# Placing the previous image's steps by hand in a two-layer FNO and dilation kernel

## The chip, the core and the metric

The kernel runs on one core of one Trainium2 chip. The metric is device time in microseconds (us) of one execution. Four runs of the kernel before the change took 3962.23 to 3968.06 us, with a median of 3965.28 us.

## The reference

`x` has 8 images of 8 channels and 256 x 256 pixels, in float32. The channels form 4 groups of 2 (`G` = 4). Two residual layers are applied:

```python
x = x + L0(_gn(x))                    # _gn: normalise each image by groups of 2 channels
x = x + max_3x3(_gn(x))               # dilation, the border counts as -2

def L0(x):                            # a Fourier neural operator, separate for each of 4 groups
    h = gconv1x1(concat(x, gridx, gridy), fc0_w, fc0_b)       # 4 -> WID = 10 channels per group
    for i in range(4):
        xf = rfft2(h)
        # keep 24 rows kx (12 lowest, 12 highest) x 12 columns ky; mix the 10 channels at each mode
        h1 = irfft2(einsum(xf_kept, sp_w1[i] or sp_w2[i]))
        h = h1 + gconv1x1(h, w_w[i], w_b[i])
        if i < 3: h = gswish(h, betas[i])                     # h * sigmoid(h * softplus(beta)) / 1.1
    h = gswish(gconv1x1(h, fc1_w, fc1_b), betas[3])           # 10 -> 128 channels per group
    return gconv1x1(h, fc2_w, fc2_b)                          # 128 -> 2 channels per group
```

## The kernel before

**Two streams of work.** All matmuls are float32. Image by image the program does a latent part, `layers(b, ...)`, which holds the state `h` (30 rows of each 32 partitions in use, 11 chunks of 4 x 512 columns) in SBUF, and a head, `head(b, ...)`, which reads the last state back from DRAM and applies fc1, the activation and fc2. The head of image b-1 is cut into 128 steps (`STEPS`), which are laid between the pieces of the latent part of image b; the head of the last image runs alone at the end. The dilation of a finished image is a third, thin stream of pieces, called tails here (`dilate`, lines 730 to 766).

**A head step.** `first(n)` (L674) makes 4 matmuls (8 instructions, L680) into 4 PSUM banks, and ACT applies Silu to them in two instructions (L681, one bank; L682, three banks). Every odd step also calls `second(n - 3)` (L685): 8 matmuls (16 instructions, L702) over the activations of steps n-3 and n-2 into one bank, which DVE adds to the output `y` (L707, or L705 for the first of a block). Before a block of three steps, `load_state` (L667) has SP fetch a chunk of the state; at the first pair of a block of 16, SP fetches `y` (L695); after the last pair POOL writes `y` to DRAM (L715). A tail is a few DVE instructions on two rows (L748 to L764); its input `yin` comes and its output goes by POOL's queue.

**PSUM.** Two pools share the 8 banks: `one` (2 buffers of one bank) and `tri` (2 buffers of three banks). A step takes one of each, an odd step a second `one`; so does nearly every piece of the latent part, by `ps_a`, `ps_tri` or `ps_four` (both).

**A layer of the latent part.** `spectrum_h` (L341): four DVE transposes (L347) turn the gathered coefficients `zt`, then 96 matmul instructions make `p_b` (L356), and DVE scales it into `B` (L363). `mix` (L376): twelve DVE instructions of 800 elements, alternately a multiplication (L383) and a reduction (L386), mix the channels at each mode; two more make `F`; matmuls fold the result (`p_f`, L403) and four copies of 32 partitions each put it into the diagonal places of `fz` (L416 to L419, by `copy`, L196, which gives every second copy to ACT while no head exists). `rows_of` (L421): matmuls turn `fz` into row coefficients (`p_g`, L435 or L440) and ten copies bring them into `zt`. `layer` (L458): for each of 11 chunks `burst` (L504) adds the 1x1 convolution (L511 or L514) and the inverse transform (L517) in 4 banks, and ACT writes the chunk back (L522, or L524 in the last layer). In layers 0 to 2 the chunks are taken in pairs k: `turn` (L461) transposes a chunk on DVE in two halves (L465), `transform(k)` (L472) makes `p_d` from a pair (L482; copied out by DVE, L485, and ACT, L486), and `gather(k)` (L488) makes `p_u` (L496) and copies it into `zt` (L499, L502). In layer 3 nothing is turned, and SP writes each chunk to DRAM (`stored`, L526).

**The next image's start.** `spectrum_x` (L242) normalises x and computes its spectrum with a DFT by matmuls: `p_a` (L283, L289, L296), then `p_xs` (L307), where 64 small matmuls (128 instructions) unfold the half spectrum, group by group, into 4 banks. `mix(b + 1, 0)` follows. These form `start(b + 1)`; layer 3 of image b advances it by one yield at each `next(side)` (L455, L544, L546), and what is then left runs at the image's end (L608).

**What sets the order.** PE, DVE and ACT run in program order (`manual_schedule`, L789); SP and POOL issue DMAs in an order that the scheduler picks. In the main loop (L796 to L813) each yield of the latent part says what goes in there. A tuple is an exact number of steps. A plain number is a weight: it is scaled (L814) so that an image has 128 steps, and a step is placed when the shares add up to one. `"odd"` and `"even"` insert a step when the parity is wrong. `"tail"` places one tail. A head is created after the whole of `layers(b)`, the start of b+1 included (L820).

Of the kernel before, what the change touches and what calls it, by code (L numbers as in the profile page):

```python
# [21 lines left out]
G = 4  # L22
# [21 lines left out]
def fno_dilate_kernel(ctx: ExitStack, tc: tile.TileContext, a: dict, out: bass.AP):  # L44
# [78 lines left out]
    nc.vector.memset(fz, 0.0)  # L123

# [117 lines left out]
    def spectrum_x(b, out_):  # L242
# [36 lines left out]
        a1, a2, a3 = turned[:, 2, 0:512], turned[:, 2, 512:1024], turned[:, 2, 1024:1072]  # L279
# [18 lines left out]
        nc.vector.tensor_copy(a3, p[:, 0:48])  # L298
        yield
        yield  # L300
        a3 = a3.rearrange("p (j k) -> p j k", j=2)
        one, tri, banks = ps_four(f"p_xs_{b}")
        for k in range(2):
            for term in range(2):
                for q in range(4):
                    for g in range(G):
                        mm(banks[g][part(q), 6 * k : 6 * k + 6], unf[part(g), spectrum_table(k, term), :],  # L307
                           a3[part(g), :, 12 * term + 3 * q : 12 * term + 3 * q + 3],
                           start=term == 0, stop=term == 1)
        xe4 = xe.rearrange("p (s k) g j -> p s g j k", s=2)  # L310
        for k in range(2):
            nc.vector.tensor_copy(
                xe4[:, k, 0, 0:2, :], one[:, 6 * k : 6 * k + 6].rearrange("p (j k) -> p j k", j=2))
            nc.vector.tensor_copy(
                xe4[:, k, 1:4, 0:2, :], tri[:, :, 6 * k : 6 * k + 6].rearrange("p g (j k) -> p g j k", j=2))
# [25 lines left out]
    def spectrum_h(b, l, out_):  # L341
# [3 lines left out]
        for g in range(G):  # L345
# [3 lines left out]
            yield 1.2  # L349
# [26 lines left out]
    def mix(b, l, out_):  # L376
# [3 lines left out]
        for k in range(3):  # L380
            for k2 in range(2):
                pr = turned[:, 2, 1024 * k2 : 1024 * k2 + 800].rearrange("p (g m i) -> p g m i", g=G, i=WID)
                nc.vector.tensor_tensor(  # L383
                    pr, sw[k], bt[:, k2, k].unsqueeze(2).to_broadcast([128, G, 2 * WID, WID]), ALU.mult)
                yield 0.7
# [4 lines left out]
                if k == 0 and k2 == 1:  # L390
                    sw.append(load_sw(l, 2))
                yield 0.7
# [3 lines left out]
        yield 0.5  # L396

        yield "odd"
        p = ps_tri(f"p_f_{b}_{l}")[:, 0, :]
        for slot in range(2):  # L400
            for n, (table, part_of) in enumerate(((0, slot), (1 + slot, 1 - slot))):
                for q in range(4):
                    mm(p[part(q), 120 * slot : 120 * slot + 120], fold[part(q), table, :],  # L403
                       f[part(q), part_of].rearrange("p k g o -> p (k g o)"), start=n == 0, stop=n == 1)
# [11 lines left out]
        for q in range(4):  # L416
            dst = fz[part(q), :, :, 6 * q : 6 * q + 6].rearrange("p o g k -> p k g o")
            src = p[part(q), :240].rearrange("p (k g o) -> p k g o", g=G, o=WID)
            copy(q, dst, src)  # L419

    def rows_of(b, l, side):  # L421
# [3 lines left out]
        for os_ in (range(0, 4), range(4, 8), range(8, 10)):  # L425
# [25 lines left out]
            yield (1, 1) if os_[0] == 0 else (1,)  # L451
            if l < 3:
                yield "tail"
            elif os_[0] < 8:
# [3 lines left out]
    def layer(b, l, out_, stored, side):  # L458
# [79 lines left out]
        if l == 3:  # L538
            yield "odd"
            for c in range(NCH):  # L540
# [4 lines left out]
                yield (1,)  # L545
                next(side, None)  # L546
            return
        yield "even"
        for k in range((NCH + 1) // 2):
            c = 2 * k  # L550
            burst(c)
            if k > 1:
                gather(k - 2)
            if alone[0]:
                turn(c)
                if c + 1 < NCH:
# [3 lines left out]
                if c + 1 < NCH:  # L560
                    turn(c + 1)
                yield (1, 1)
                continue
            yield (1,)
            turn(c, (0,))
            if k > 0:
                transform(k - 1)
            turn(c, (1,))
            yield "tail"
            if c + 1 < NCH:  # L570
                burst(c + 1)
                turn(c + 1, (0,))
                yield (1,)
                turn(c + 1, (1,))
                yield "tail"
            else:
                yield (1,)
# [3 lines left out]
        yield 2  # L581
        gather(k)
        yield 1

    def start(b, out_):
        if b < n_img:
            out_["sw"] = [load_sw(0, 0), load_sw(0, 1)]
            yield from spectrum_x(b, out_)
            for i, n in enumerate(mix(b, 0, out_)):
                if isinstance(n, str):  # L590
                    yield n
                elif i % 2:
                    yield 1.4

    def layers(b, stored, d, then):
# [4 lines left out]
        for l in range(4):  # L600
# [6 lines left out]
            yield from layer(b, l, d, stored, then)  # L607
        yield from then  # L608
# [51 lines left out]
    def head(b, stored, stats):  # L660
# [58 lines left out]
        load_state(1)  # L719
# [270 lines left out]
```

## Time and profile before

| what | value |
|---|---|
| median of 4 runs | 3965.28 us |
| the profiled execution's own time | 3965.84 us |
| its span, first to last instruction | 3964.0 us |
| PE busy | 3673.8 us (93%) |
| ACT busy | 2832.7 us (71%) |
| DVE busy | 2457.7 us (62%) |
| PE weight loads (PEld) | 1432.9 us (36%) |
| POOL busy | 117.0 us (3%) |

The first `p_f` of image 1 starts at 362.0 us; up to there no head runs. From image to image the same point then comes after 471.8, 472.8, 472.8, 472.9, 474.1 and 476.9 us. The last chunk of image 7 ends at 3653.8 us, and the remaining head steps and the last dilation take the last 310 us.

In a busy column a matmul that is held back by a PSUM bank in the middle of its group is counted as busy, so PE's 93% holds waiting too. The timeline shows it as a group that takes longer than the same group elsewhere.

### The profile page before, as it was taken

To read this page: it belongs to the slowest core of one execution; us is meant where nothing else is said; L and a number is where in the kernel's file an instruction comes from. 1 tells how busy PE (TensorE), PEld (TensorE's weight loads), DVE (VectorE), ACT (ScalarE), POOL (GpSimd) and SP (SyncE) were. 2 spreads that over 40 slices of the span, in tenths; PEclk is the share of its full clock that TensorE was granted. 3 is DMA by queue.
4 is the path that set the end of the run, shared out by engine and by line. 5 is a ranking of instruction groups with operands and counts; after the bars stand their busy time and mean duration, and the time that the engine had idled before them with its cause. 6 is when DMAs were issued, how large, how long until landed. Compare 5 with 4: busy or idle time off the path is not lost.

```text
span 3964.0 us, 118698 instructions
## 1 busy us (share of the span) xinstructions
PE 3673.8 (93%) x53882; PEld 1432.9 (36%) x53882; DVE 2457.7 (62%) x3740; ACT 2832.7 (71%) x2933; POOL 117.0 (3%) x202
## 2 busy tenths in 40 slices
PE   5667999999999999999999999999999999999997
PEld 2333333333333333333433333333333333333222
DVE  6664656556765666756666576665776566763633
ACT  2434777777777777777777777776777767778886
POOL 1000000000000000000000000000000000000100
PEclk8888999999999999999999999999999999999998
DMA  3014111432215221251222512134211432215311
GB/s 86 15 35 173 54 32 49 138 124 68 61 56 178 88 68 59 82 188 56 61 65 96 190 48 60 59 131 147 67 53 55 169 107 60 67 49 190 100 52 47
DMA packets 114128, 345.05 MB, mean 87 GB/s; under 512 B 16040, under 2 KB 18536, under 8 KB 98200
## 3 DMA queue, kind: packets, MB, share of 16 engines
q1 hardware_dynamic: 95432, 276.32, 22.1%
q0 software_dynamic: 18192, 61.13, 4.6%
q8 instruction: 424, 6.95, 0.7%
q14 instruction: 80, 0.66, 0.1%
HBM read 213.39 MB, written 123.74 MB: 85 GB/s over the span
## 4 chain that ended last, share of the span: by engine, by line
PE 74%; DVE 13%; ACT 6%; issue 5%; DMA 1%; POOL 0%; SPq 0%; DVEq 0%; POOLq 0%; ACTq 0%
PE p_fc L680 19%; PE p_fc L702 19%; PE p_z L517 9%; PE p_d L482 7%; PE p_z L514 7%; ACT h L522 3%; PE p_z L511 2%; PE p_b L356 2%; DVE turned L347 2%; PE p_u L496 2%; DVE turned L465 2%; PE p_g L435 2%; PE p_g L440 2%; DVE S L386 2%; DVE y L707 2%
## 5 line engine op out<-in xcount | busy, mean ns | idle before, releaser
L682 ACT ACTIVATE act<-p_fc 128x1536 f32<-128x1536 f32 x1024 | 1492.0, 1457 | 2.9 <-PE p_fc L680 2.9
L680 PE MATMUL p_fc<-hs,c_w 32*128 32x512 f32 x8192 | 1166.0, 630 | 12.9 <-DVE h L705 6.1
L702 PE MATMUL p_fc<-act,c_w 128*32 128x512 f32 x8192 | 990.9, 601 | 0.4 <-issue 0.4
L681 ACT ACTIVATE act<-p_fc 128x512 f32<-128x512 f32 x1024 | 615.5, 601 | 450.8 <-PE p_fc L680 439.9
L465 DVE STREAM_TRANSPOSE turned<-h 128x1024 f32<-128x1024 f32 x528 | 646.9, 1234 | 290.0 <-ACT h L522 290.0
L522 ACT ACTIVATE h<-p_z 128x512 f32<-128x512 f32 (+1 forms) x528 | 511.9, 1021 | 261.6 <-PE p_z L517 261.6
L680 PEld LDWEIGHTS p_fc<-hs,c_w 32*128 32x128 f32 x8192 | 387.6, 185 | 551.2 <-ACT act L681 209.6
L707 DVE TENSOR_TENSOR y<-p_fc,y 128x512 f32<-128x512 f32 x392 | 266.2, 679 | 445.9 <-PE p_fc L702 445.9
L702 PEld LDWEIGHTS p_fc<-act,c_w 128*32 128x32 f32 x8192 | 215.5, 109 | 705.9 <-issue 395.8
L517 PE MATMUL p_z<-c_binv,zt 32*128 32x256 f32 x5632 | 410.7, 406 | 3.1 <-ACT zt L198 1.8
L514 PE MATMUL p_z<-h,c_wt 32*32 32x512 f32 x8448 | 388.3, 603 | 18.4 <-DVE zt L200 7.7
L517 PEld LDWEIGHTS p_z<-c_binv,zt 32*128 32x128 f32 x5632 | 259.1, 187 | 312.1 <-issue 298.5
L482 PE MATMUL p_d<-turned,c_fw 32*32 32x480 f32 (+1 forms) x9216 | 327.8, 541 | 17.3 <-DVE zt L499 5.1
L524 ACT ACTIVATE h<-p_z,c_bias 128x512 f32<-128x512 f32 (+1 forms) x176 | 186.6, 1111 | 108.0 <-PE p_z L517 107.7
L486 ACT ACTIVATE turned<-p_d 128x1440 f32<-128x1440 f32 x144 | 183.1, 1271 | 107.4 <-PE p_d L482 104.2
L200 DVE COPY zt<-p_g 128x264 f32<-128x264 f32 x300 | 162.0, 616 | 90.8 <-PE p_g L435 50.4
L482 PEld LDWEIGHTS p_d<-turned,c_fw 32*32 32x32 f32 x9216 | 127.3, 103 | 212.6 <-issue 64.4
L386 DVE TENSOR_REDUCE S<-turned 128x80 f32<-128x800 f32 x192 | 188.8, 984 | 5.2
L383 DVE TENSOR_TENSOR turned<-t,B 128x800 f32<-128x800 f32 x192 | 188.4, 981 | 1.2 <-DMA t<-in_spw 1.0
L347 DVE STREAM_TRANSPOSE turned<-zt 128x960 f32<-128x960 f32 x96 | 174.5, 1852 | 1.8
L514 PEld LDWEIGHTS p_z<-h,c_wt 32*32 32x32 f32 x8448 | 96.5, 103 | 214.4 <-ACT act L681 70.8
L485 DVE COPY turned<-p_d 128x480 f32<-128x480 f32 x144 | 88.6, 615 | 137.6 <-PE p_d L482 136.7
(179 smaller groups left out, 1991.4 us busy)
## 6 DMA issues: line engine op xcount, KB each, us to landing
stored<-h SPq DMA_DIRECT2D x88, 1024.0 KB
hs<-stored SPq DMA_DIRECT2D x352, 256.0 KB
t<-in_spw SPq DMA_DIRECT2D x96, 400.0 KB
yin<-y_rows POOLq DMA_DIRECT2D x56, 512.0 KB, 5.2
h<-in_xp SPq DMA_DIRECT2D x352, 48.0 KB
turned<-in_xw SPq DMA_DIRECT2D x16, 1024.0 KB
y<-in_x SPq DMA_DIRECT2D x56, 256.0 KB
y_rows<-y POOLq DMA_DIRECT2D x56, 256.0 KB, 2.3
```

The costliest lines, as they stand in the source:

```text
L347: nc.vector.transpose(rows[:, 960 * g : 960 * (g + 1)].rearrange("p (i r) -> p i r", r=32), windows(g))
L386: nc.vector.tensor_reduce(s[k2][:, k].rearrange("p g s o -> p (g s o)"), pr.rearrange("p g m i -> p (g m) i"), AX.X, ALU.add,)
L465: nc.vector.transpose(dst[:, 2 * i : 2 * i + 2], h[:, c, 2 * i : 2 * i + 2].rearrange("p f (s x) -> p f s x", s=2))
L482: mm(banks[q][part(v % 4), : 240 * n], fw8[part(q), v, :], t[part(q), :, :, v, : NBLK * WID], start=v < 4, stop=v >= 4)
L514: mm(o, wt[part(q), l, g, :], h[part(q), c, f, :], start=True, stop=False)
L517: mm(banks[q][:, HW * s : HW * (s + 1)], zt[part(q), 2 * c + s].rearrange("p f o -> p (f o)"), binv[part(q), :], start=False, stop=s == 1)
L522: nc.scalar.activation(dst, src, AF.Silu)
L680: mm(banks[g], w1[part(g), blk, :], hs[k][part(g), :], start=True, stop=True)
L681: nc.scalar.activation(act[:, 0, :], one, AF.Silu)
L682: nc.scalar.activation(act[:, 1:4, :], tri, AF.Silu)
L702: mm(acc[part(g), :], w2[:, g, 15 - rb - i : 47 - rb - i], act[:, g, :], start=i == 0, stop=i == 1)
L707: nc.vector.tensor_tensor(y, sums, y, ALU.add)
```

## The change

All weights and parity yields become fixed numbers of steps, and the head of an image is created as soon as its last layer ends, before the rest of `start(b + 1)`, with its first two loads issued at once. Steps per layer, before (as the trace shows them, images 2 to 7) and after (counted in the code):

| stretch | layers | before | after |
|---|---|---|---|
| from `p_f` to the first burst | 0, 1, 2 / 3 | 7, 7, 7 / 6 | 7, 7, 7 / 6 |
| first burst to last burst | 0, 1, 2 / 3 | 10, 10, 10 / 20 | 8, 8, 8 / 20 |
| last burst to `p_b` | 0, 1, 2 | 8, 7, 7 | 8, 8, 8 |
| `p_b` to the next `p_f` | 0, 1, 2 | 9, 8, 8 | 9, 9, 9 |
| last burst of layer 3 to the next image's `p_f` | 3 | 4 | 6 |

The steps keep their parity at each of these places. In layers 0 to 2 the first pair of chunks has no step and no tail between its pieces; in the later pairs both halves of the even chunk are turned before `transform`, and the tails (two, in pairs 2 to 4) stand behind it. In the twelve mixing instructions a step follows each but the numbers 2, 6 and 10. A layer 3 has tails in two places per chunk for six chunks, and one of its two `next(side)` in `rows_of` moves behind the last group of copies. The four copies into `fz` become one multiplication with a mask `own` over all partitions, with `p_f` laid out in `fz`'s order and taken from pool `one`. The 64 unfolding matmuls become 16, from an operand `a3` of 128 rows that holds each group's values in its own 32 rows and zeros elsewhere; the result fills one bank of pool `one`.

```diff
+    own = const.tile([128, NQ], F32, tag="own", name="own")
+    nc.vector.memset(own, 0.0)
+    for i in range(NQ):
+        nc.vector.memset(own[part(i), i : i + 1], 1.0)
...
-        a1, a2, a3 = turned[:, 2, 0:512], turned[:, 2, 512:1024], turned[:, 2, 1024:1072]
+        a1, a2 = turned[:, 2, 0:512], turned[:, 2, 512:1024]
+        a3 = turned[:, 2, 1024:1216].rearrange("p (g m) -> p g m", g=G)
+        nc.vector.memset(a3, 0.0)
...
-        nc.vector.tensor_copy(a3, p[:, 0:48])
+        for g in range(G):
+            nc.vector.tensor_copy(a3[part(g), g, :], p[part(g), 0:48])
...
-        one, tri, banks = ps_four(f"p_xs_{b}")
+        p = ps_a(f"p_xs_{b}")
         for k in range(2):
             for term in range(2):
                 for q in range(4):
-                    for g in range(G):
-                        mm(banks[g][part(q), 6 * k : 6 * k + 6], unf[part(g), spectrum_table(k, term), :],
-                           a3[part(g), :, 12 * term + 3 * q : 12 * term + 3 * q + 3],
-                           start=term == 0, stop=term == 1)
+                    k0 = 12 * term + 3 * q
+                    mm(p[part(q), 24 * k : 24 * k + 24], unf[:, spectrum_table(k, term), :],
+                       cols[:, :, :, k0 : k0 + 3], start=term == 0, stop=term == 1)
...
-            yield 1.2
+            yield (1,) if g < G - 1 else (1, 1)
...
+            if l > 0:
+                if n not in (2, 6, 10):
+                    yield (1,)
+            elif n % 2 or n > 7:
+                yield (1,)
...
-        yield "odd"
-        p = ps_tri(f"p_f_{b}_{l}")[:, 0, :]
+        p = ps_a(f"p_f_{b}_{l}")
...
-        for q in range(4):
-            dst = fz[part(q), :, :, 6 * q : 6 * q + 6].rearrange("p o g k -> p k g o")
-            src = p[part(q), :240].rearrange("p (k g o) -> p k g o", g=G, o=WID)
-            copy(q, dst, src)
+        nc.vector.tensor_tensor(
+            fz[:, :, :, : 6 * NQ].rearrange("p o g (q k) -> p (o g) q k", q=NQ),
+            p[:, : 6 * WID * G].rearrange("p (n k) -> p n k", k=6).unsqueeze(2).to_broadcast([128, WID * G, NQ, 6]),
+            own.unsqueeze(1).unsqueeze(3).to_broadcast([128, WID * G, NQ, 6]), ALU.mult)
...
-            yield (1, 1) if os_[0] == 0 else (1,)
+            yield (1, 1) if os_[0] == 0 or os_[0] == 8 and l < 3 else (1,)
             if l < 3:
                 yield "tail"
-            elif os_[0] < 8:
+            elif os_[0] != 4:
                 next(side, None)
...
-            if alone[0]:
+            if k == 0 or alone[0]:
                 turn(c)
...
-                yield (1, 1)
                 continue
             yield (1,)
-            turn(c, (0,))
-            if k > 0:
-                transform(k - 1)
-            turn(c, (1,))
-            yield "tail"
-            if c + 1 < NCH:
+            turn(c)
+            transform(k - 1)
+            for _ in range(2 if k > 1 and pair else 1):
+                yield "tail"
+            if pair:
                 burst(c + 1)
                 turn(c + 1, (0,))
-                yield (1,)
+            yield (1,)
+            if pair:
                 turn(c + 1, (1,))
-                yield "tail"
-            else:
-                yield (1,)
         out_["sw"] = [load_sw(l + 1, 0), load_sw(l + 1, 1)]
         gather(k - 1)
         transform(k)
-        yield 2
+        yield (1,)
         gather(k)
-        yield 1
...
             yield from layer(b, l, d, stored, then)
+        yield "stored"
         yield from then
...
         load_state(0)
         load_state(1)
+        yield
...
+                if n == "stored":
...
+                    heads.append((b, head(b, stored, stats_of[b])))
+                    next(heads[-1][1])
+                    alone[0] = False
+                elif n == "tail":
+                    tail()
+                elif heads:
+                    for _ in n:
                         step()
```

## The prediction

> **What bounds the kernel now.** The page comes first: busy shares, then the chain that ended last.
>
> ```profile
> PE 3673.8 (93%) x53882; PEld 1432.9 (36%) x53882; DVE 2457.7 (62%) x3740; ACT 2832.7 (71%) x2933; POOL 117.0 (3%) x202
> ...
> PE 74%; DVE 13%; ACT 6%; issue 5%; DMA 1%; POOL 0%; SPq 0%; DVEq 0%; POOLq 0%; ACTq 0%
> ```
>
> PE is the bound in images 1 to 7 and DVE is what it waits for. The number of steps doesn't change, so only PE's waiting can move. The waits by releaser, then the timeline of PE and of DVE, say where it waits:
>
> ```profile
> PE p_f L403 <- DVE F L394: 97.1, 18, 15.5
> PE p_b L356 <- DVE turned L347: 40.9, 22, 7.5
> ...
> PE p_z L514 <- DVE zt L200: 7.7, 6, 1.3
> ```
>
> ```profile
> 1534.08 3.75 PE L356 MATMUL p_b<-turned,c_eh_f 128*32 128x120 f32 x96 [1.56 <-DVE turned L347]
> ...
> 1582.88 1.04 PE L680 MATMUL p_fc<-hs,c_w 32*128 32x512 f32 x8
> 1583.85 1.92 PE L702 MATMUL p_fc<-act,c_w 128*32 128x512 f32 x16
> 1585.71 1.16 PE L514 MATMUL p_z<-h,c_wt 32*32 32x512 f32 x32
> ...
> 1695.92 1.15 PE L514 MATMUL p_z<-h,c_wt 32*32 32x512 f32 x30 [1.29 <-DVE zt L200]
> ...
> 1751.12 2.54 PE L514 MATMUL p_z<-h,c_wt 32*32 32x512 f32 x31
> ...
> 1779.43 1.02 PE L403 MATMUL p_f<-F,c_fold 32*32 32x120 f32 x32 [4.13 <-DVE F L394]
> ...
> 1840.37 2.16 PE L482 MATMUL p_d<-turned,c_fw 32*32 32x480 f32 x60 [0.66 <-DVE zt L502]
> ```
>
> ```profile
> 1692.34 2.46 DVE L248 BATCH_NORM_STATS2 bn_x<-turned 128x6 f32<-128x512 f32 x4
> 1694.72 1.05 DVE L200 COPY zt<-p_g 128x264 f32<-128x264 f32 x2
> ...
> 1875.18 0.75 DVE L705 SCALAR_TENSOR_TENSOR y<-p_fc,c_b,y 128x512 f32<-128x512 f32 x1 [2.75 <-PE p_fc L702]
> 1875.85 3.68 DVE L347 STREAM_TRANSPOSE turned<-zt 128x960 f32<-128x960 f32 x2
> ...
> 1903.53 0.69 DVE L707 TENSOR_TENSOR y<-p_fc,y 128x512 f32<-128x512 f32 x1 [0.49 <-PE p_fc L702]
> 1904.13 0.27 DVE L394 TENSOR_TENSOR F<-S,S 128x120 f32<-128x120 f32 x1
> ```
>
> The starts of 1582.88 to 1585.71 give a step's price on PE: 0.97 us for the first part, 1.86 for the second, so an odd step costs 2.83. The DVE rows show the cause of most waits: DVE runs in order, an odd step's add (0.69) can't start before PE's second part ends, and everything behind it waits (at 1875.18 DVE stood idle for 2.75 us with four transposes queued).
>
> **The change part by part**, per image unless said; plus is faster. Where steps move between stretches, each is credited at its PE price, so the terms add up.
>
> *Last burst to `p_b`.* From `p_u` of pair 4 to `p_b` layer 0 now takes 16.05 us (1867.82 to 1883.87) with 6 first parts and 3 second parts, layers 1 and 2 take 14.6 (1519.50 to 1534.08) with 5 and 2. Now a step stands before the first transpose, and its add holds all four back. After, none does: `p_u` 0.95, `p_d` 1.4, a step 0.97, `p_u` 0.6, then five steps (4.85 + 3 x 1.86 = 10.4) and 0.5 for ACT, whose two instructions (601 + 1457 ns) are slower than a step's PE part: 14.8 with 6 and 3. DVE needs a copy 0.41, four transposes of 1.85 and two adds, 9.2, beside the 10.4. Gain 1.25 + 2 x (14.6 + 2.83 - 14.8) = 6.5; bounds 4 (`p_b` waits 0.8 in each) and 7.
>
> *Mixing, `p_b` to `p_f`.* Now the last add stands right before `F`: 16.95 us from the end of `p_b` (1887.6 to 1904.56) in layer 0, 16.35 and 17.3 in layers 1 and 2. After, four odd steps end at 4 x 3.96 = 15.85 (a pair of steps by the L680 starts 1887.53, 1891.50, 1895.49), the add of the last runs to 16.6, and behind it stand two mixing instructions (1.95) and `F` (0.5): `p_f` at 19.1, with only one even step to cover it. Layer 0 loses 2.15; layers 1 and 2, which take one first part more, lose 1.75 and 0.8: -4.7. Bounds -6 and -3.5. So part of what is won before `p_b` comes back before `p_f`.
>
> *Pairs 1 to 5.* At 1840.37 a tail of five DVE instructions stood between the last half transposition and the copies of `p_u`, so `p_d` waited. Summed over the 84 such places, the step ahead of `p_d` advances 20.0 us more than 0.97 each. The moved tails leave the copies first: +2.6 of 2.86; lower bound 1.5.
>
> *First pair without steps.* Now from the first `p_z` to the end of `p_d` of pair 0 takes 15.1 us, of which 4.8 are steps. After, three bursts run at ACT's pace (2.05 each), one step follows, and `p_d` waits for the second chunk's transposes to 9.1: 11.2 with 1.0 of steps. Nothing gained, nothing lost; what was a wait for ACT becomes one for DVE.
>
> *Folding.* Four copies take 2.3 us; one multiplication of 960 elements 1.15 (between 981 ns for L383's 800 and 1201 for L748's 1024). Beside steps this shows little: `p_f` leaves pool `tri`, whose bank held the next step (1.1 us in layer 1), but the second part now waits for the multiplication to free `one`. `p_f` to `p_g`: 5.95, 5.35, 4.9 become 5.1 each: +0.7 (0 to 0.9). In image 0 ACT and DVE take the copies in turn with nothing beside them: 4 x 1.2 = 5 once.
>
> *Rows of layer 3.* Four bn_stats (2.46) stood before the last copies; behind them the first burst starts at 1693.8, not 1695.9: +2.1 in six images.
>
> *Unfolding.* The burst behind it took 2.54 where 1.15 is free, since `p_xs` held a `tri` bank: that goes. The nearest row for the new form is L440 (128 instructions of 128x32 by 66 columns in 1.98 us), 0.5 for 32; the other end is today's 1.66. So the burst ends at 1751.1 to 1752.3, not 1753.7: +1.8 (1.4 to 2.6), six images. DVE's memset and three more copies (about 0.2 each, from L298's 207 ns) stand beside steps. Against this stands the Trainium skill, "TensorEngine Tiling (Array Packing)", "Performance Considerations": tile the rows where the contraction is 32, up to 4x, and don't count on fewer columns below 60. By it a quarter of the matmuls at a quarter of the concurrency would save nothing, and the term would be 1.4, and the gain 2 us less in all; no row shows this form at 24 columns.
>
> *More tails in layer 3* may hold a `one` bank: -0.5.
>
> *Hand-over.* The new head's five steps come among the last four mixing instructions and `F`. From the last burst (1767.1): second parts of steps 124 and 126 to 4.8, step 0 to 5.8; step 1 needs the bank of step 126's sum, whose add stands behind five mixing instructions, so it waits to 10.2; `p_f` comes at 18.1 instead of 12.3, and with seven steps in `rows_of` the next layer's first burst at 40.3 instead of 36.8. That is 3.5 later with 2 first parts and 1 second part more (3.8): 0, bounds -5 and +3. What is queued: SP's loads of a new head are no risk, since SP's timeline has the first issued at 1757.9 for a step at 1786.8, and the stored chunks lie in DRAM long before; the load of `y` must wait until POOL has written the last block (add, 0.69, issue 0.54, landing 2.3) and lands about when it is needed. In image 0 the 7.7 us between last burst and `p_f` take five steps: +3 once. Image 7 has no start: three steps fewer run alone, +0.7.
>
> **The sum**: 7 x (6.5 - 4.7 + 2.6 + 0.7) = 35.7; 6 x (2.1 + 1.8 - 0.5) = 20.4; 5 + 3 + 0.7 = 8.7: 65 us. The profiled execution's own time is 3965.84 (span 3964.0), 0.6 above the median: 3965.8 - 65 = 3901, against the median 3900. With all lower bounds (the tails of layer 3 at -1) the gain is 7 x (4 - 6 + 1.5) + 6 x (2.1 + 1.4 - 1 - 5) + 5 = -14, 3979; with all upper ones 7 x (7 - 3.5 + 2.9 + 0.9) + 6 x (2.1 + 2.6 + 3) + 8.7 = 106, 3859. The terms are independent, so this case's own range is 3868 to 3938.
>
> **Rivals.** *A. The hand-over stalls* (bank, `y`, two second parts in a row): 5.5 us in six images, 3933 to 3940. For: DVE's add is 5 us behind PE there. Against: PE waits 4.13 there already. *B. Nothing is gained*: the copies, adds and transposes only wait elsewhere, as in the first pair, and the mixing loses 6: 3965. Against: 2.1 and 1.8 are tied to single banks and instructions. *C. Slower.* In pairs 2 to 4 two tails now stand together between `p_d`'s copy and the odd chunk's transposition, 63 places. DVE has 3.05 us there (copied at 7.35, ACT done at 10.4 after the pair's start) and two tails take 2.4 to 3.3, more if `yin` (5.2 us to landing) is late; the transposition, the add and the next `p_d` then slip. It decides from 65 / 63 = 1.03 us a place; at 1.6 the time is 4000. Against: behind the transposes `p_d` has another 1.3 us. That the steps move as the code says leaves no doubt.
>
> **How the numbers follow.** Forecast 0.62, A 0.13, B 0.07, C 0.18. A change of 0.2% (8 us) is about what a measurement of this kernel can tell. Faster is the forecast and A, 0.75; same 0.07; slower 0.18. For 8 in 10 the range goes from the forecast's low end over A and B into C's weak end: 3866 to 3985.
>
> **What would show it.** Right: `p_b` no longer waits for `turned`; `p_f` in the mixing waits about 2.2 us for `F` in every layer; the burst behind `p_xs` takes 1.2; 472.8 us an image become about 464. Wrong: `p_d` waiting for `turned` in pairs 2 to 4, or over 45 us from the last burst to the next image's first.

## The result and the profile after

The changed kernel takes 3974.6 us (median) against 3968.1 us for the kernel before in the same comparisons: ratio 1.0019, 95% interval 1.0014 to 1.0025. The prediction was 3900 us. About 70 us of expected gain are missing. The profiled execution's own time is 3972.05 us, its span 3970.2 us.

First the busy time and the chain that ended last, from the page of the changed kernel:

```profile
PE 3680.4 (93%) x53114; PEld 1427.2 (36%) x53114; DVE 2442.7 (62%) x3675; ACT 2829.5 (71%) x2923; POOL 117.0 (3%) x202
...
PE 79%; DVE 11%; issue 4%; ACT 4%; DMA 2%; POOL 0%; DVEq 0%; SPq 0%; POOLq 0%; ACTq 0%
```

PE has 768 instructions less than before and is busy 6.6 us longer. Something that PE does has become slower; this is the first thing to look for. Then the waits of the changed kernel by releaser (us in total, times, longest):

```profile
PE p_f L415 <- DVE F L405: 86.0, 27, 13.1
...
PE p_d L494 <- DVE turned L477: 23.2, 18, 1.4
...
PE p_fc L686 <- DVE y L713: 21.4, 6, 9.4
...
DVE turned L390 <- DMA t<-in_spw: 18.9, 8, 7.3
...
PE p_b L362 <- DVE turned L353: 15.0, 2, 7.5
...
PE p_z L523 <- DVE wcn L549: 14.1, 7, 3.4
```

`p_b` waits only in image 0 now, as forecast. `p_f` waits almost as long as before, but as 27 waits instead of 18: the hand-over's 4.13 us are gone and each mixing has 2.13 us instead. Two lines were in no forecast: the first burst of layer 0 waits for `wcn`, and a mixing instruction on DVE waits for a DMA, the spectral weights. That a step waits for an add on `y` was in the hand-over's term, as a wait of 4.4 us (5.8 to 10.2); it takes 1.2 to 9.4.

Last the timeline of PE, then of DVE, around one mixing (layer 3, image 3), and the same place by windows (the column after the engines is the granted clock of TensorE):

```profile
1667.00 1.14 PE L686 MATMUL p_fc<-hs,c_w 32*128 32x512 f32 x8
1670.27 1.96 PE L415 MATMUL p_f<-F,c_fold 32*32 32x120 f32 x32 [2.13 <-DVE F L405]
1672.16 1.85 PE L686 MATMUL p_fc<-hs,c_w 32*128 32x512 f32 x8
```

```profile
1667.14 0.75 DVE L711 SCALAR_TENSOR_TENSOR y<-p_fc,c_b,y 128x512 f32<-128x512 f32 x1 [0.66 <-PE p_fc L708]
1667.80 0.98 DVE L390 TENSOR_TENSOR turned<-t,B 128x800 f32<-128x800 f32 x1
1668.82 0.99 DVE L393 TENSOR_REDUCE S<-turned 128x80 f32<-128x800 f32 x1
1669.84 0.28 DVE L405 TENSOR_TENSOR F<-S,S 128x120 f32<-128x120 f32 x1
```

```profile
1668.00:1670.00 2.00, 0.14 (x4) 0.00 (x0) 1.93 (x3) 1.84 (x2) 0.00 (x0) 1.00 0.78 250
1670.00:1672.00 2.00, 1.73 (x32) 1.36 (x32) 0.42 (x3) 0.09 (x1) 0.00 (x0) 0.56 0.52 182
1672.00:1674.00 2.00, 2.00 (x18) 0.58 (x16) 1.16 (x1) 0.00 (x0) 0.00 (x0) 0.59 0.00 0
1674.00:1680.00 6.00, 6.00 (x163) 2.96 (x160) 2.36 (x5) 3.88 (x5) 0.00 (x0) 1.00 0.20 49
```

Three things can be read here. The add, two mixing instructions and `F` stand behind PE's last odd step, as the prediction said, and PE idles 2.13 us. `p_f` takes 1.96 us where the row of before had 1.02. And behind the wait the clock is granted at a half for some 3.4 us, so the next step's first part takes 1.85 us instead of 1.14.

By stretch, mean over images 1 to 7, from the starts in the two timelines. The net column credits every moved first part with 0.97 us and every second part with 1.86, as the prediction did; plus is faster:

| stretch | before | after | net gain an image | predicted |
|---|---|---|---|---|
| last burst to `p_b`, layers 0 to 2 | 66.8 | 66.1 | +6.4 | +6.5 |
| `p_b` to `p_f`, layers 0 to 2 | 61.8 | 68.3 | -4.6 | -4.7 |
| first to last burst, layers 1 and 2 | 112.85 | 103.9 | +1.3 | +1.7 of 2.6 |
| first to last burst, layer 0 | 57.2 | 56.8 | -3.4 | +0.9 of 2.6 |
| `p_f` to first burst, layers 1 and 2 | 44.8 | 47.9 | -3.1 | about 0 |
| `p_f` to the end of the first burst, layer 3 (6 images) | 22.8 | 22.3 | +0.5 | +2.1 |
| rest of layer 3 (6 images) | 70.0 | 67.0 | +3.0 | +1.3 |
| last burst to the next image's first (6 images) | 37.35 | 44.5 | -3.3 | 0 |

The first `p_f` of image 1 comes 4.3 us earlier (357.7; in the kernels below whose hand-over of image 0 is the same it comes between 351.5 and 359.8, so a difference of this size can be the execution's), the end behind the last burst is 13.2 us shorter (128 lone steps instead of 132), and images 1 to 7 together take 23.7 us longer: 6.2 us in the span.

### The profile page after: what moved, and what is told of

Same layout as the page of the kernel before. It is cut to its first block, busy times and chain, and to the rows that moved or that the text cites. A ratio compares the mean times of both kernels' runs of the same rounds, so it can differ in the third digit from the quotient of the medians.

```text
span 3970.2 us, 116980 instructions
## 1 busy us (share of the span) xinstructions
PE 3680.4 (93%) x53114; PEld 1427.2 (36%) x53114; DVE 2442.7 (62%) x3675; ACT 2829.5 (71%) x2923; POOL 117.0 (3%) x202
## 4 chain that ended last, share of the span: by engine, by line
PE 79%; DVE 11%; issue 4%; ACT 4%; DMA 2%; POOL 0%; DVEq 0%; SPq 0%; POOLq 0%; ACTq 0%
PE p_fc L686 22%; PE p_fc L708 21%; PE p_z L529 9%; PE p_d L494 7%; PE p_z L526 6%; PE p_z L523 3%; PE p_u L508 3%; DVE turned L477 2%; PE p_b L362 2%; PE p_g L452 2%; PE p_g L447 2%; PE p_f L415 2%; DVE turned L390 1%; DVE turned L353 1%; DMA t<-in_spw 1%
## 5 line engine op out<-in xcount | busy, mean ns | idle before, releaser
L686 PE MATMUL p_fc<-hs,c_w 32*128 32x512 f32 x8192 | 1180.9, 643 | 46.2 <-DVE y L713 21.4
L477 DVE STREAM_TRANSPOSE turned<-h 128x1024 f32<-128x1024 f32 x528 | 630.0, 1224 | 318.0 <-ACT h L534 317.7
L686 PEld LDWEIGHTS p_fc<-hs,c_w 32*128 32x128 f32 x8192 | 378.7, 187 | 624.9 <-ACT act L687 227.7
L529 PE MATMUL p_z<-c_binv,zt 32*128 32x256 f32 x5632 | 420.0, 413 | 0.0
L526 PE MATMUL p_z<-h,c_wt 32*32 32x512 f32 x8448 | 353.8, 599 | 6.2 <-ACT act L687 4.1
L494 PE MATMUL p_d<-turned,c_fw 32*32 32x480 f32 (+1 forms) x9216 | 310.9, 541 | 23.5 <-DVE turned L477 23.2
L415 PE MATMUL p_f<-F,c_fold 32*32 32x120 f32 x1024 | 62.2, 391 | 101.9 <-DVE F L405 86.0
```

The costliest lines, as they stand in the source:

```text
L477: nc.vector.transpose(dst[:, 2 * i : 2 * i + 2], h[:, c, 2 * i : 2 * i + 2].rearrange("p f (s x) -> p f s x", s=2))
L494: mm(banks[q][part(v % 4), : 240 * n], fw8[part(q), v, :], t[part(q), :, :, v, : NBLK * WID], start=v < 4, stop=v >= 4)
L526: mm(o, wt[part(q), l, g, :], h[part(q), c, f, :], start=True, stop=False)
L529: mm(banks[q][:, HW * s : HW * (s + 1)], zt[part(q), 2 * c + s].rearrange("p f o -> p (f o)"), binv[part(q), :], start=False, stop=s == 1)
L686: mm(banks[g], w1[part(g), blk, :], hs[k][part(g), :], start=True, stop=True)
```

## The experiments

All are edits of the changed kernel. A ratio is to the kernel before; a difference to the changed kernel is the difference of the two ratios times 3968 us.

### The order of the steps in the mixing

```diff
             if l > 0:
-                if n not in (2, 6, 10):
-                    yield (1,)
+                if n % 3 != 1:
+                    yield (1, 1) if n == 11 else (1,)
```

> After with one edit: in the mixing of layers 1 to 3 the nine steps stand after instructions 0, 2, 3, 5, 6, 8, 9 and 11, with two after 11, so that an odd step's add follows each third instruction and the last add stands right before F with an even step behind it. Theory (the order of the adds on DVE): in the changed kernel an add, two mixing instructions and F remain when PE has only one even step left, so p_f waits 2.13 us in each of 21 mixings; here p_f should wait 0.3 to 0.6 us, the way from p_b to p_f should fall from 22.8 to about 21.2 us, and the time should lie 21 x 1.6 = 34 us below the changed kernel. Theory with the clock: 18 of these 21 waits are followed by 3.4 us at half the granted clock; if the waits fall under 1 us those stretches should vanish and up to 0.8 us more come back at each, 15 us in all: 34 to 50 us below. Rival (DVE is full): the twelve instructions, six scalings and four adds bound the mixing by themselves, the wait only moves to an earlier place: within 10 us of the changed kernel.

Measured: 3919.4 us, ratio 0.9875 (0.9862 to 0.9888), 57 us below the changed kernel. `p_b` to `p_f` takes 20.9 us in every layer instead of 22.8, and the wait of `p_f` in all falls from 86.0 to 46.6 us. The PE timeline and one DVE line of the new kernel at the same mixing:

```profile
1640.48 1.14 PE L686 MATMUL p_fc<-hs,c_w 32*128 32x512 f32 x8
1641.84 1.94 PE L415 MATMUL p_f<-F,c_fold 32*32 32x120 f32 x32 [0.23 <-DVE F L405]
1643.71 1.14 PE L686 MATMUL p_fc<-hs,c_w 32*128 32x512 f32 x8
```

```profile
1640.77 0.74 DVE L711 SCALAR_TENSOR_TENSOR y<-p_fc,c_b,y 128x512 f32<-128x512 f32 x1
1641.42 0.27 DVE L405 TENSOR_TENSOR F<-S,S 128x120 f32<-128x120 f32 x1
```

Nothing but `F` stands behind the last add now, and DVE is not full: it idles in front of the earlier adds. The gain is 18 us more than the 39 us of waiting, and none of the 21 mixings is followed by a half clock (in the changed kernel 19 of 21 are, not the 18 of the expectation). `p_f` still takes 1.94 us, so its slowness is not the clock's.

### Is the half clock a cost of its own?

```diff
+        if l > 0:
+            for _ in range(5):
+                for q in range(4):
+                    mm(p[part(q), 0:120], eh_f[:, 0, 0, :], binv[:, 0:120], start=True, stop=True)
         sums = p[:, : 6 * WID * G].rearrange(...)
```

> After with one addition: ahead of p_f in layers 1 to 3, PE runs 40 matmul instructions of p_b's kind (about 1.5 us by p_b's row) into p_f's own bank, whose values p_f then overwrites, so that PE is busy through most of the wait for F. Nothing becomes ready sooner. Theory (the clock): the changed kernel loses time twice at p_f, by the wait and by the 3.4 us at half the granted clock behind 18 of the 21 waits; the even mixing won 55 us with only 39 us less of waiting, so some 10 to 18 us should come back here though p_f starts no earlier, and no half-clock stretch should stand behind p_f. Rival (the rest of those 55 us came from elsewhere, such as a better order of banks): no change within 4 us, or a loss if the filler delays p_f.

Measured: 3959.1 us, ratio 0.9973 (0.9963 to 0.9984), 18 us below the changed kernel, although nothing becomes ready sooner and PE has 840 instructions more. The same mixing in the PE timeline:

```profile
1649.10 1.14 PE L690 MATMUL p_fc<-hs,c_w 32*128 32x512 f32 x8
1650.17 1.23 PE L414 MATMUL p_f<-c_binv,c_eh_f 128*32 128x120 f32 x40
1652.29 1.94 PE L419 MATMUL p_f<-F,c_fold 32*32 32x120 f32 x32 [0.88 <-DVE F L405]
```

The way from `p_b` to `p_f` stays at 22.7 us; the half clock follows 3 of 21 mixings instead of 19 (this one is among the three), and layers 1 to 3 from `p_f` to the first burst give back 11.6 us. The rest of the 18 lies in places that the edit does not touch (image 0 and the hand-over, 6 and 3 us in the profiled execution), which differ between executions; so 12 us are shown to be the clock's, and the rest may be.

### The form of `p_f`

```diff
-        f = sb.tile([128, 2, 3, G, WID], F32, tag="F", ...)
+        fo = sb.tile([128, 2, 3, WID, G], F32, tag="F", ...)
+        f = fo.rearrange("p s k o g -> p s k g o")
...
-                    mm(sums[part(q), slot], fold[part(q), table, :],
-                       f[part(q), part_of].rearrange("p k g o -> p o g k"), start=n == 0, stop=n == 1)
+                    mm(p[part(q), 120 * slot : 120 * slot + 120], fold[part(q), table, :],
+                       fo[part(q), part_of].rearrange("p k o g -> p (k o g)"), start=n == 0, stop=n == 1)
...
-            p[:, : 6 * WID * G].rearrange("p (n k) -> p n k", k=6).unsqueeze(2)...
+            p[:, : 6 * WID * G].rearrange("p (k n) -> p n k", k=6).unsqueeze(2)...
```

> After with one edit: F is written by DVE in the order (k, o, g), p_f reads it and writes its bank in unbroken rows of 120 columns, and the one masked multiplication reads the bank with a stride instead. Theory (form of the matmul): p_f's group takes 1.94 us since its operand and its result are strided; here it should take 1.02 us as in the kernel before, and the time should fall by 28 x 0.92 = 26 us, less what the multiplication (1.16 us) gets longer by the stride. Rival (the clock): p_f is slow since it follows a wait of 2.13 us and runs at half the granted clock; then the group stays at 1.8 to 1.94 us here and the time does not move.

Measured: 3948.9 us, ratio 0.9943 (0.9929 to 0.9956), 30 us below the changed kernel; the groups of `p_f` alone give back 20.8 us (62.2 to 41.4 below). The wait in front of them is 2.22 us here, no shorter than 2.13, but only 10 of 21 are followed by a half clock instead of 19. Which of the two strides costs was asked by a second kernel, in which the bank is written in unbroken rows and F is read with a stride:

```diff
-                    mm(sums[part(q), slot], fold[part(q), table, :],
-                       f[part(q), part_of].rearrange("p k g o -> p o g k"), ...)
+                    mm(p[part(q), 120 * slot : 120 * slot + 120], fold[part(q), table, :],
+                       f[part(q), part_of].rearrange("p k g o -> p k o g"), ...)
```

> After with p_f's bank written in unbroken rows and only its operand F still read with a stride (the folding in unbroken rows read both without: 1.02 us a group against 1.94). Theory (writing in runs of three costs): p_f takes 1.02 us here. Rival (reading with a stride costs): 1.94. Both: something between.

It took 3973.5 us in its one run. The groups of `p_f` by line and shape (busy us, mean ns of one instruction), first of the changed kernel, then of the kernel in unbroken rows, then of the one that only reads with a stride:

```profile
L415 PE MATMUL p_f<-F,c_fold 32*32 32x120 f32 x1024 | 62.2, 391 | 101.9 <-DVE F L405 86.0
```

```profile
L415 PE MATMUL p_f<-F,c_fold 32*32 32x120 f32 x1024 | 41.4, 309 | 106.5 <-DVE F L406 90.2 <-issue 15.6 <-PE p_fc L686 0.7
```

```profile
L414 PE MATMUL p_f<-F,c_fold 32*32 32x120 f32 x1024 | 60.6, 385 | 102.7 <-DVE F L405 86.6 <-issue 15.6
```

It is the read. The moving operand is the one that is not loaded as weights, here F. When its neighbours are not neighbours in memory, a group takes 1.94 us, or 1.88 to 1.91 when the result is written in unbroken rows; when they are, it takes 1.02 at full clock (the mean of 309 ns holds groups at half clock too, which take 1.82). The masked multiplication takes its strided operand from PSUM without harm (1153 ns in both kernels). With this out of the way the folding is what the prediction meant it to be: `p_f` to the first burst takes 21.5 us at best in layer 1 (22.2 before, 23.2 after).

### The scaling in front of layer 0

```diff
             own.unsqueeze(1).unsqueeze(3).to_broadcast([128, WID * G, NQ, 6]), ALU.mult)
+        if l == 0:
+            wcn = sb.tile([128, 32], F32, tag="wcn", bufs=1, name=f"wcn_{b}")
+            nc.vector.tensor_scalar(wcn, wc, out_["mr"][:, 1:2], None, ALU.mult)
+            out_["wcn"] = wcn
...
         if l == 0:
             for c in range(NCH):
                 read_x(c)
-            wcn = sb.tile([128, 32], F32, tag="wcn", bufs=1, name=f"wcn_{b}")
-            nc.vector.tensor_scalar(wcn, wc, out_["mr"][:, 1:2], None, ALU.mult)
+            wcn = out_["wcn"]
```

The place in the changed kernel, image 5, on DVE and on PE:

```profile
2283.64 0.69 DVE L713 TENSOR_TENSOR y<-p_fc,y 128x512 f32<-128x512 f32 x1 [3.20 <-PE p_fc L708]
2284.25 1.22 DVE L757 TENSOR_TENSOR m<-m,yin 128x1024 f32<-128x1024 f32 x1
2285.38 0.23 DVE L549 TENSOR_SCALAR wcn<-wc,mr_x 128x32 f32<-128x32 f32 x1
```

```profile
2285.76 1.15 PE L523 MATMUL p_z<-h,wcn 6*32 6x512 f32 x32 [2.19 <-DVE wcn L549]
2286.85 1.15 PE L529 MATMUL p_z<-c_binv,zt 32*128 32x256 f32 x16
2287.92 2.05 PE L523 MATMUL p_z<-h,wcn 6*32 6x512 f32 x32
2289.91 2.09 PE L529 MATMUL p_z<-c_binv,zt 32*128 32x256 f32 x16
```

The change closes `rows_of` with an odd step and a tail. The add and the tail stand ahead of an instruction of 0.23 us, and the first burst waits for that. From 2288 on the clock is granted at 0.50 and the next bursts take 4.1 us instead of 2.3; it lasts to 2298, through the first pair, which has no step. That the missing steps make it last is not shown by a run of its own.

> After with one edit: the small scaling of the first layer's weight (wcn, one DVE instruction of 0.24 us) is made right behind the masked multiplication instead of after all rows. Theory (a queue behind an add): in the changed kernel wcn stands behind an odd step's add and a tail, the first burst of layer 0 waits for it 14.1 us in seven images, and where the wait is over 2 us the granted clock falls to a half for 7 to 14 us, in which a burst takes 4.1 us instead of 2.3; both should go: 14 us of waits and 3 to 5 us in each of four images, 25 to 32 us below the changed kernel, with layer 0 from first to last burst at 53 to 54 us in all images. Without the clock's part: 14 us. Rival (the rows or the bank are late anyway): the first burst waits for zt or a bank instead, less than 5 us.

Measured: 3934.2 us, ratio 0.9916 (0.9904 to 0.9927), 41 us below the changed kernel, more than expected. In the profiled execution `p_f` to first burst in layer 0 gives back 14.6 us in seven images and first to last burst 11.3, which is the 26 of waits and clock; 12 more lie in image 0 and in the hand-over, which differ between executions, so how much of these 12 is the edit's own is not shown. Layer 0 still takes 51.9 to 57.1 us from first to last burst, not 53 to 54 in all.

### The hand-over

> After with one edit: the new head is created behind the rest of the next image's start, as in the kernel before, so the last steps of the old head stand between the last mixing instructions and the new head begins at p_f. Theory (hand-over): in the changed kernel PE waits 1.2 to 9.4 us an image there for an add that is queued behind mixing instructions, and these instructions wait 18.9 us in all for the spectral weights, whose load is issued late by SP; here the way from the last burst to p_f should go back from 18.4 us on the mean to 15 or 16, with 1 to 5 us of half clock less, 15 to 35 us below the changed kernel. Rival (the stall only moves to the next layer's rows, where second parts of the old head now stand): within 8 us of the changed kernel.

```diff
-        yield "stored"
         yield from then
+        yield "stored"
```

Measured: 4182.7 us, ratio 1.0542 (1.0526 to 1.0558), 208 us above the changed kernel. This is not the hand-over: in all layers of all images the time rises (layers 1 and 2 first to last burst 55.2 us instead of 52.0, layer 3 81.9 instead of 69.5), because the first head starts five steps later and every odd step stands where an even one stood. A lone step in image 0 was meant to mend it:

```diff
                     alone[0] = False
+                    if b == 0:
+                        step()
```

> The head created behind the next image's start, as before in this study, and with one lone step of the first head at once. Without that step the kernel took 208 us more than the changed one: its first head begins five steps later, so every place in the program gets an odd step where the changed kernel has an even one. Theory (parity): with the parity put back the bursts of layers 1 and 2 take 52.0 us again from first to last and not 55.2, layer 3 about 69.5 and not 81.9, and the time is within 25 us of the changed kernel, 10 to 20 below it if the hand-over is better there. Rival (the later creation itself: states fetched too late, second parts of the old head in the next rows): it stays over 4100 us.

Measured: 4157.3 us, ratio 1.048 (1.0464 to 1.0495). Image 1 has the changed kernel's stretches again (52.1, 52.0, 52.0 us) and takes 466.7 us. There the first head is used up one step early, the second starts with the wrong parity, and images 2 to 6 take 502 to 511 us. So neither expectation held for the whole kernel, and it is seen why. With the lone step in every image but the last (`if b + 1 < n_img:`):

> The head created behind the next image's start, and one step of it at once in every image but the last, so that odd and even steps stand at the changed kernel's places in every image (with the lone step in image 0 alone, image 1 took 466.7 us from p_f to p_f, and the later images fell back to the turned parity and about 505). Theory (parity alone made the loss): all images now take 465 to 475 us and the time is near the changed kernel's 3974.6. Of the hand-over itself: the old head's last second parts stand there instead of the new head's, the new head's y is needed later; if the changed kernel's hand-over stalls (1.2 to 9.4 us an image) come from the new head, 10 to 25 us below it; if they come from the mixing's queue and SP's loads, which are unchanged, within 8 us of it. Rival (late creation costs by itself): above 3990.

Measured: 3985.1 us, ratio 1.0044 (1.0031 to 1.0058), 10 us above the changed kernel. So parity made 198 of the 208 us, and the order of old and new head is not what makes the hand-over slow; the old place is slightly worse.

What makes it slow was in the waits: DVE waits for the third block of spectral weights. DVE's timeline of the worst case in the changed kernel:

```profile
3200.03 0.99 DVE L393 TENSOR_REDUCE S<-turned 128x80 f32<-128x800 f32 x1
3208.31 0.99 DVE L390 TENSOR_TENSOR turned<-t,B 128x800 f32<-128x800 f32 x1 [7.30 <-DMA t<-in_spw]
3209.22 0.68 DVE L713 TENSOR_TENSOR y<-p_fc,y 128x512 f32<-128x512 f32 x1
```

The load can't be issued before the first block's buffer is free, which it was at 3192.71, when the second multiplication ended. SP's timeline, and its waits from 3180 to 3216 us, show what held it up:

```profile
3191.95 6.51 SPq L542 DMA_DIRECT2D h<-in_xp  x4
3198.57 0.35 SPq L538 DMA_DIRECT2D stored<-h  x1
3201.07 0.61 SPq L379 DMA_DIRECT2D t<-in_spw  x1
```

```profile
SPq L542 <- DMA stored<-h: 22.7, 5, 7.0
```

SP stood in its reads of the next image's x, which wait for stored chunks of the state, and came to the weights 8.4 us late; the multiplication could start 7.2 us after that. PE's next step waits for the add behind it, 9.37 us. The load is issued 3.3 to 8.4 us late at five of the seven hand-overs of the changed kernel, and at most 0.43 us late at the seven of the kernel before. At the other two it is issued in time and is still waited for (2.8 and 1.4 us).

```diff
         nc.vector.tensor_copy(a1, p)
+        out_["sw"].append(load_third(0))
...
+    def load_third(l):
+        t = turned[:, 1, 0:800]
+        nc.sync.dma_start(t, a["spw"][l, 2])
+        return t.rearrange("p (g m i) -> p g m i", g=G, i=WID)
...
-            if n == 3:
+            if n == 3 and l > 0:
                 sw.append(load_sw(l, 2))
```

> After with one edit: the third block of spectral weights of the next image's layer 0 is loaded into a part of the x buffer that is free by then, and issued right behind the first DFT matmuls instead of behind the fourth mixing instruction. Theory (a late load): in the changed kernel the ninth mixing instruction waits 18.9 us in eight images for this load, 7.3 in image 6, and PE stands behind it 9.4 us; here these waits go under 3 us in all, the last burst of layer 3 to p_f falls from 18.4 us on the mean (16 to 24) to about 15.5 in every image, and the time by 10 to 20 us. Rival (the adds and mixing instructions on DVE are the longer chain): the way to p_f falls by less than 1 us an image, and the time by less than 6 us.

Measured: 3946.7 us, ratio 0.9944 (0.9932 to 0.9956), 30 us below the changed kernel, more than the 10 to 20 expected. The wait for the weights is gone from the profile, last burst to `p_f` takes 14.9 us on the mean (14.2 to 16.7) instead of 18.4 (15.6 to 23.9), which is 21 us in six images, and the first `p_f` of image 1 comes at 350.0 instead of 357.7, much of which other kernels show without this edit. The wait of steps for `y` in images 1 to 7 falls from 21.4 to 4.9 us.

### The unfolding of x

The old form put back: 64 matmuls, group by group, into four banks.

```diff
-        p = ps_a(f"p_xs_{b}")
+        one, tri, banks = ps_four(f"p_xs_{b}")
         for k in range(2):
             for term in range(2):
                 for q in range(4):
-                    mm(p[part(q), 24 * k : 24 * k + 24], unf[:, spectrum_table(k, term), :], ...)
+                    for g in range(G):
+                        mm(banks[g][part(q), 6 * k : 6 * k + 6], unf[part(g), spectrum_table(k, term), :], ...)
```

> After with the unfolding of x undone: 64 small matmuls group by group into four banks, as in the kernel before. The prediction's term: the burst behind it then waits for a bank again, 1.4 to 2.6 us in six images, 1.8 taken: 8 to 16 us above the changed kernel, and layer 3 from first to last burst about 71 us instead of 69.5. Rival (the steps hide it): no change within 4 us. Rival (fewer columns cost as much as more matmuls, so that only the bank matters): the same time of p_xs's group, 1.7 us, in both.

Measured: 3978.8 us, ratio 1.0027 (1.0017 to 1.0036), 3 us above the changed kernel, which can hardly be told from nothing. The trace can tell: from the start of `p_xs` to the end of the burst behind it is 4.32 us in this kernel and 2.99 in the changed one, 1.33 in each of six images, 8 us. The matmuls themselves take 0.45 us there instead of 1.5. The Trainium skill's rule that the prediction weighed ("TensorEngine Tiling (Array Packing)", "Performance Considerations": tile rows where the contraction is 32) does not hold at this size: 32 instructions over 128 rows take 0.45 us, 128 over 32 rows 1.5.

### Together

The even mixing, the folding in unbroken rows and the early `wcn`:

> After with three edits at once: steps spread evenly in the mixing, folding in unbroken rows, wcn made early. Alone they won 55, 26 and 40 us against the changed kernel's 3974.6. Theory (three separate places): the gains add up to 121 us, 3850 to 3860 us. Rival (they overlap: the same half-clock stretches and the same slack at the hand-over are counted in more than one of them): 90 to 110 us, 3865 to 3885. In either case a kernel faster than both by more than 2%.

Measured: 3858.0 us, ratio 0.9719 (0.9706 to 0.9732), 119 us below the changed kernel; alone they gave 57, 30 and 41. Then the early weights as a fourth:

> After with four edits at once: the three of the mended kernel before (even mixing, folding in unbroken rows, wcn early; together 117 us below the changed kernel, at 3858) and the early third block of spectral weights, which alone won 28 us. Theory (four separate places): 3825 to 3835 us. Rival (wcn early and the early weights both take away the same half-clock stretches and the same slack between the hand-over and layer 0's first burst): 3835 to 3850. No wait of DVE for the spectral weights over 2 us, and no way from the last burst to p_f over 17 us, in either case.

Measured: 3829.7 us, ratio 0.9657 (0.9643 to 0.9670): 144 us below the changed kernel and 136 below the kernel before. The separate gains add up to 158, so the four are nearly independent. They are more than the 70 us that were missing: about 33 of them are the loss in the mixing that the prediction had counted (7 x 4.7), and how much of the rest the kernel before lost too is not shown. Busy time and waits of PE in this kernel:

```profile
PE 3600.1 (94%) x53114; PEld 1405.4 (37%) x53114; DVE 2436.7 (64%) x3675; ACT 2829.3 (74%) x2923; POOL 117.4 (3%) x202
```

```profile
PE p_f L421 <- DVE F L412: 47.1, 27, 13.2
PE p_d L504 <- DVE turned L487: 26.3, 21, 1.4
```

PE does the same instructions as in the changed kernel in 80 us less. From the first `p_f` of image 1 to the last burst of image 7 the clock that was not granted (one minus the granted share, summed over the time) comes to 11.9 us, against 81.9 in the changed kernel and 31.7 before.

## Why the prediction was wrong

The forecast case (a gain of 65 us) failed, and so did its sign; that the time still lies in the range of 3866 to 3985 is luck, since the range reached that far for rival C, which did not happen. The terms that were worked out from waits and queues mostly hold. Four steps failed, in places that the prediction had priced at nothing or had not looked at: the strided read of `p_f` (30 us by its own run), the queue in front of `wcn` (41), the late third load of spectral weights at the hand-over (30), and the half clock behind a wait (12 to 18).

*Last burst to `p_b`*: right, +6.4 for +6.5. *Mixing*: right, -4.6 for -4.7; `p_f` waits 2.13 us in all 21 mixings (2.2 foreseen). But the step took the wait as the whole price. The half clock behind it costs at least 12 us more (filler), and the even order wins 57 us where the wait alone is worth 39. The profile of before had the hint: behind the 4.13 us waits at the hand-over its granted clock falls to a half too.

*Pairs 1 to 5*: right in layers 1 and 2, +0.67 each for 0.87. *First pair without steps*: "nothing gained, nothing lost" failed in layer 0. In five of seven images the half clock comes there and stays for 10 to 14 us, through the whole pair. The step moved into `rows_of` (the odd one at its end) was counted on PE, but not on DVE, where its add and the tail stand ahead of `wcn`: the sum had no term for what stands behind a moved add. The early `wcn` is worth 41 us by its own run, 26 of them in layer 0.

*Folding*, +0.7 an image: the multiplication was sized right (1.16 us for 1.15), but the prediction looked only at what replaces the copies. The same edit made `p_f` read F with a stride, and `p_f` went from 1.02 to 1.94 us. That is the failed step of the term: 30 us by its own run. With it mended `p_f` to `p_g` takes 5.2 us in layers 1 to 3, for the 5.1 foreseen.

*Rows of layer 3*, +2.1: only +0.5 is seen, since `p_f`'s 0.92 us and the half clock lie in the same stretch. With those mended the stretch takes 20.8 us, 2.0 less than before: the term was right, and covered. *Unfolding*, +1.8: mis-sized, 1.33; the matmuls' time was right, 0.45 us for 0.5. *Rest of layer 3*: 1.7 us an image beyond the unfolding were gained and are not explained.

*Hand-over*: the prediction named a chain of bank, add and mixing instructions, and said of SP's queue only that a new head's loads are no risk. The load that mattered is the third block of spectral weights, which SP now issues up to 8.4 us late, behind its reads of the next x. Last burst to the next image's first takes 44.5 us for the 40.3 foreseen; with the weights early or `wcn` early alone it takes 41, with all four edits 37.8. Rival A (the hand-over stalls) was therefore right in kind and not in mechanism. Rival C (two tails together) is out: first to last burst in layers 1 and 2 is 52.0 us in all 14 cases, and `p_d` waits in the first pair alone. Rival B named the right size by the wrong means: not because nothing was gained, but since gains and losses are both large.

*Parity*: that the steps move as the code says was right, and that they keep their parity weighs more than any term of the sum: 198 us.

## What to carry to other kernels

When a piece of work is moved, follow its instructions on every engine, and ask in each in-order queue what small thing now stands behind them; a 0.23 us scaling behind an add and a tail was worth 41 us. Do the same for SP: a load stands behind whatever SP waits for ahead of it. When a copy is replaced, look at the access pattern of the matmul that feeds it as well as at the copy. A wait of PE of 2 us has a second price behind it, which waits of 1.5 us did not have here.

## What the runs showed of the hardware

A strided moving operand costs these small float32 matmuls (32x120, 32 instructions) nearly half their rate at full clock and almost nothing at half clock: 1.93 to 1.96 us at either clock when F is read in steps of 40 elements, against 1.02 at full and 1.82 at half clock when it is read in unbroken rows. Writing PSUM in runs of three costs next to nothing (62.2 us busy with it, 60.6 without). Writing was suspected as much as reading before the runs.

The granted clock falls to a half for 3.4 us, or two to four times as long, mostly after PE has idled. In the fourteen profiles of this study, from the first `p_f` of image 1 to the last burst of image 7, none of 206 idle stretches of 1.4 to 1.6 us that began at full clock was followed by a half clock within 3.4 us; of 184 of 2.0 to 2.6 us, 143 were, and all 61 of 2.6 us and more. But so were 64 of 146 of 1.0 to 1.4 us, so the length of one stretch is not the whole rule. The Trainium skill ("TensorE: Matmul & The Clock Gate", "HAM oscillation — how this bites in real kernels") warns of gaps above about 3.4 us; here 3.4 us is the length of a slow stretch, and gaps of 2.1 us were followed by one in 19 of the changed kernel's 21 mixings. Filling most of these waits with useless matmuls left 3 of 21 and made the kernel 18 us faster.

One and the same load is waited for 0.8 to 7.3 us at the seven hand-overs of one execution of the changed kernel. Its runs lie between 3963 and 3987 us, the five runs with the weights loaded early and the other three edits between 3829 and 3834; whether the load makes this difference is not shown.
